# Layer norms of a conv-and-scan kernel's second stage: statistics by broadcast matmuls replaced by transposes and VectorE's batch-norm instructions

## The chip, the cores and the metric

One Trainium2 chip; the kernel runs on one of its cores. The time is device microseconds for one execution of the whole kernel. The engines are TensorE (PE in the profile, its weight loads PEld), VectorE (DVE), ScalarE (ACT), GpSimd (POOL) and SyncE (SP, which issues DMAs).

## The reference

A tensor of 4 images, 192 channels, 64 x 64 positions goes through four layers. Layer 0 is a norm, two Mamba scans and a residual; layer 2 is a dynamic depthwise convolution and layer 3 a windowed sedenion product with an MLP. The change lies in layer 1 alone, cut here to its frame:

```python
t = _ln(transpose(x, (0, 2, 3, 1)), ln1_g, ln1_b)        # norm 1, over the 192 channels
y = _mamba(t.reshape(B, 4096, 192), ...)                 # projections, 3 taps, scan over 4096 positions
x1 = x + back(y)
x2 = x1 + _gelu(batch_norm(depthwise_conv3x3(x1)))
t = _ln(transpose(x2, (0, 2, 3, 1)), ln2_g, ln2_b)       # norm 2, over the 192 channels
out = x2 + back(_gelu(t @ w1 + b1) @ w2 + b2)            # MLP, 192 -> 768 -> 192
# _ln: (x - mean) * rsqrt(var + 1e-5) * g + b, mean and variance over the last axis
```

## The kernel before

`program` runs three stages one after the other. `two_mambas` is layer 0. `mamba_block` is layer 1, called the second stage here. `conv_and_windows` is layers 2 and 3; it is a generator whose first part (batch 0's convolution and norms) is ticked along while the second stage drains.

**Tiles.** The second stage takes 32 tiles, 8 to an image, of 512 positions each. Channels lie on partitions: a tile is [96, 2, 512], two halves of 96 channels. The scan of a tile is 48 steps: 12 groups `k` of four `j`. Each step is one VectorE scan over [128, 512] (L654, `Mamba.step`); ScalarE makes its decay `dA` by an Exp two steps ahead (L648, `decay`, three PSUM buffers); a group begins with a product [128, 2048] (L641), on VectorE, or on GpSimd for groups 3, 7 and 11 ("apart"); it ends with a product by C on GpSimd (L667, `read`), and TensorE gathers the result (L676, `sum`).

**What sets the order.** Each engine works through its own queue in the order of the program, and the program's order is made by the class `Behind`. After each scan step `Behind.tick` issues other work of the stage "behind" the scan. That work is written as generators in five lanes, tried in the order of their numbers: lane 0 the way out of the scan (`back`, with the residual sum into `strip`, L1102) and C's spreading; lane 1 a tile's projections and taps (`front`) and norm 1; lane 2 `tail` (the 3 x 3 convolution as 18 matmul pairs, its gelu, norm 2); lane 3 `end` (the MLP); lane 4 a silu. What a generator yields is a `Piece`: the TensorE time `pe` of the next part, set against a budget of 1.8 a step; the steps to `wait`; flags `after` which it may go; `bank`, since only two PSUM banks are shared by all lanes; `act`, ScalarE's time, set against 1.4 a step; `burst` for long activations (gelu, silu, softplus), which go only two steps before the end of a group that a VectorE product follows; and `lock`, one holder at a time. `Behind.later` puts off the reading of a PSUM bank by one step on ScalarE (`act`) or two on VectorE (`dve`). A deferred reading with an `act` is issued only while the step's ScalarE account is above zero; a Piece that is no burst goes when its `act` is at most 0.84 or the account, whichever is larger, so small pieces go even when the account is negative.

**A norm before** (`NormT.run`, L300 to L356) keeps channels on partitions. TensorE multiplies by a matrix of 1/192 to get the mean on all 96 partitions (`mean`, L307); VectorE subtracts it (L309); ScalarE squares (L316); TensorE sums the squares into [128, 4] (`var`, 8 products with one moving column each, L321); ScalarE adds epsilon (L332) and GpSimd raises to the power -0.5 (L333); TensorE spreads the result back to channels (`rb`, L339); VectorE multiplies (L347); ScalarE applies g and b (L354, twice). On TensorE each f32 product shows as two matmul instructions. The lock is held from after the subtraction to the end of `var`, since `ln_sq` has one buffer.

In each tile there is one norm 1, of the tile two ahead, and one norm 2, at the end of `tail`: 64 norms in all. Norm 2's first product waits for `taken`: `MlpT.run` sets it once the MLP of the tile before has read the one buffer `xn2`. `end` then follows. A `tail` starts when its tile's `back` and the `end` of an older tile are done.

The first stage has a norm of its own (L840 to L890), whose rows are of use below: its input has positions on partitions, ScalarE does its passes (L861) on [128, 192], GpSimd small steps on [128, 4] (L865 to L871), TensorE transposes [128, 96] blocks with one instruction each (L879), and ScalarE reads the result with g and b (L883).

Of the kernel before, what the change touches and what calls it, by code (L numbers as in the profile page):

```python
# [14 lines left out]
F32 = mybir.dt.float32  # L15
AF = mybir.ActivationFunctionType
ALU = mybir.AluOpType
# [5 lines left out]
C = 192  # L23
# [262 lines left out]
class NormT:  # L286


    FIRST = dict(pe=1.7, bank=True)

    def __init__(self, nc, const, work, behind):
        self.nc, self.work, self.behind = nc, work, behind
        self.mean_w = const.tile([CP, CP], F32, name="mean_w")
        nc.vector.memset(self.mean_w, 1.0 / C)
        self.eps = const.tile([128, 1], F32, name="eps")
        nc.vector.memset(self.eps, EPS)
        self.minus_half = const.tile([128, T // 128], F32, name="minus_half")
        nc.vector.memset(self.minus_half, -0.5)
        self.ident = const.tile([128, 128], F32, name="ident")
        make_identity(nc, self.ident)  # L300

    def run(self, x, g, b, d, which):
        nc, behind = self.nc, self.behind
        nq = T // 128
        mean = behind.bank([CP, T], "mean")
        for k in range(2):
            nc.tensor.matmul(mean, self.mean_w, x[:, k, :], start=(k == 0), stop=(k == 1))  # L307
        h = behind.later(
            lambda: nc.vector.tensor_tensor(  # L309
                d, x, mean.unsqueeze(1).broadcast_to([CP, 2, T]), ALU.subtract  # L310
            ),
            dve=True,
        )
        yield Piece(after=[h], wait=3, act=1.05, lock=True)
        sq = self.work.tile([CP, 2, T], F32, name="ln_sq", bufs=1)
        nc.scalar.activation(sq, d, AF.Square)  # L316
        yield Piece(2.5, wait=2, bank=True)
        var = behind.bank([128, nq], "var")
        for q in range(nq):
            for k in range(2):  # L320
                nc.tensor.matmul(  # L321
                    var[:, q : q + 1],
                    sq[:, k, bass.ts(q, 128)],
                    self.mean_w[:, 0:1],
                    start=(k == 0),
                    stop=(k == 1),
                )
        behind.locked = False
        rs = self.work.tile([128, nq], F32, name="ln_rs", tag=f"ln_rs{which}", bufs=1)

        def power():
            nc.scalar.activation(rs, var, AF.Identity, bias=self.eps)  # L332
            nc.gpsimd.tensor_tensor(rs, rs, self.minus_half, ALU.pow)  # L333

        h = behind.later(power, act=0.25)
        yield Piece(1.3, after=[h], wait=4, bank=True)
        rb = behind.bank([CP, T], "rb")
        for q in range(nq):
            nc.tensor.matmul(  # L339
                rb[:, bass.ts(q, 128)],  # L340
                rs[:, q : q + 1].to_broadcast([128, CP]),
                self.ident,
                start=True,
                stop=True,
            )
        h = behind.later(
            lambda: nc.vector.tensor_tensor(  # L347
                d, d, rb.unsqueeze(1).broadcast_to([CP, 2, T]), ALU.mult
            ),
            dve=True,  # L350
        )
        for k in range(2):
            yield Piece(after=[h], wait=0 if k else 3, act=0.8)
            nc.scalar.activation(  # L354
                d[:, k, :], d[:, k, :], AF.Identity, scale=g[:, k : k + 1], bias=b[:, k : k + 1]
            )  # L356
# [655 lines left out]
def mamba_block(tc, x, p96, p96_ap, p128, p128_ap, m_in, ex_aps, out, sums, following):  # L1012
# [4 lines left out]
    with ExitStack() as ctx:  # L1017
# [50 lines left out]
        def norm(u):  # L1068
            xn = u["xn"] = scan.tile([CP, 2, T], F32, name="xn", bufs=1)
            yield from ln.run(u["x"], w["ln1_g"], w["ln1_b"], xn, 1)  # L1070
# [48 lines left out]
        def tail(b, t):  # L1119
# [37 lines left out]
            yield Piece(1.7, bank=True, wait=4, after=[taken[0]])  # L1157
            xn = work.tile([CP, 2, T], F32, name="xn2", tag="xn2", bufs=1)
            yield from ln.run(x2, w["ln2_g"], w["ln2_b"], xn, 2)
            units[b * NT + t]["past"][0] = True  # L1160
            taken[0] = [False]
            behind.add(3, end(b, t, x2, xn, taken[0]), Piece(1.7, bank=True, wait=2))
# [28 lines left out]
        def before(n):  # L1191
            if n + 1 < len(units):
                behind.add(1, front(units[n + 1]), Piece())
            if n + 2 < len(units):
                behind.add(1, norm(units[n + 2]), Piece(1.7, bank=True, after=[units[n + 2]["loaded"]]))
# [15 lines left out]
        behind.add(1, norm(units[0]))  # L1211
        behind.add(1, front(units[0]), Piece())
        behind.add(1, norm(units[1]))
# [633 lines left out]
```

## Time and profile before

| | us |
|---|---|
| median of 3 runs (10560.6 to 10564.75) | 10563.82 |
| span of the profiled execution | 10559.3 |
| second stage, first scan (of 1536) starts | 5324.9 |
| second stage, last scan ends | 8650.5 |
| third stage's first product (L1505) starts | 8899.1 |
| three first tiles of the second stage, together | 292.1 |
| the 28 tiles after them, together | 2944.0 |
| busy in the span: PE / DVE / ACT / POOL | 8657.5 / 8765.6 / 6675.7 / 7932.4 |

The profiled execution's own time is its span and what lies around it; its span is 4.5 us under the median of the runs. A tile's time is from its first scan's start to that of the next tile. In a row of instructions the columns are line, engine, operation, tiles, shape and count, then busy time and mean ns of one, then the engine's idle time before them and what ended it. TensorE's ends are modelled, so that its busy time is not a rate.

### The profile page before, as it was taken

Reading aid. Unit: us, or ns where it says so; the run is one execution under the profiler, and the core shown is the slowest. Engines: PE = TensorE matmul, PEld = TensorE weight load, DVE = VectorE, ACT = ScalarE, POOL = GpSimd, SP = SyncE. Lnnn points to the kernel's source line nnn. Section 1 sums busy time; section 2 is a strip of 40 time slices with the busy share of each in tenths; the row PEclk is TensorE's granted clock in tenths of the full one; section 3 lists DMA queues with packets and bytes.
Section 4 is the critical chain, followed back from the end, with each engine's and each line's share of the span. In section 5 each row is a group of like instructions: output and inputs, shape, how many; then the busy total and the mean of one; then the engine's idle time right before and its main releaser. Section 6 shows DMA issues by size and latency. Waiting matters only on the chain. (4 is left out here: it accounts for less than half of the span.)

```text
span 10559.3 us, 96732 instructions
## 1 busy us (share of the span) xinstructions
PE 8657.5 (82%) x30648; PEld 3478.9 (33%) x30648; DVE 8765.6 (83%) x7569; ACT 6675.7 (63%) x9690; POOL 7932.4 (75%) x3712
## 2 busy tenths in 40 slices
PE   6777777877877777787668888888888996889898
PEld 2222222322322222222223333333333333545555
DVE  7999999999999999999878887887888876555552
ACT  5776777667777667767456676776776653434443
POOL 6999999999999999999778887888888861101100
PEclk7888888888888888888668898998998987999999
DMA  6666666666666666666555554555555543122110
GB/s 163 183 187 180 178 183 186 178 181 188 182 179 183 183 181 180 185 182 179 143 143 148 134 153 131 152 138 143 141 149 135 149 109 74 42 56 59 41 41 19
DMA packets 969559, 1515.09 MB, mean 143 GB/s; under 512 B 244346, under 2 KB 277150, under 8 KB 968534
## 3 DMA queue, kind: packets, MB, share of 16 engines
q1 hardware_dynamic: 968190, 1505.85, 53.5%
q8 instruction: 243, 3.98, 0.2%
q10 hardware_dynamic: 856, 3.05, 0.1%
q14 instruction: 270, 2.21, 0.1%
HBM read 1295.45 MB, written 213.12 MB: 143 GB/s over the span
## 5 line engine op out<-in xcount | busy, mean ns | idle before, releaser
L654 DVE TENSOR_TENSOR_SCAN h<-dA,m_state,h 128x512 f32<-128x512 f32 x3328 | 4041.4, 1266 | 269.8 <-ACT dA L648 207.8
L648 ACT ACTIVATE dA<-dtE,m_A 128x512 f32<-128x512 f32 x4608 | 3101.1, 686 | 1217.6 <-DVE h L654 925.4
L667 POOL TENSOR_TENSOR h<-h,C 128x2048 f32<-128x2048 f32 x832 | 3768.3, 4529 | 71.3 <-ACT C L629 4.0
L641 DVE TENSOR_TENSOR h<-dtxE,B 128x2048 f32<-128x2048 f32 x832 | 1881.7, 2262 | 74.5 <-DMA dtxE<-r_dtx 68.1
L654 DVE TENSOR_TENSOR_SCAN h_apart<-dA,m_state,h_apart 128x512 f32<-128x512 f32 x1280 | 1551.2, 1262 | 199.9 <-ACT dA L648 190.0
L641 POOL TENSOR_TENSOR h_apart<-dtxE,Bs 128x2048 f32<-128x2048 f32 x320 | 1475.5, 4611 | 35.2 <-ACT dA L648 16.2
L667 POOL TENSOR_TENSOR h_apart<-h_apart,C 128x2048 f32<-128x2048 f32 x320 | 1449.7, 4530 | 25.8
L676 PE MATMUL y<-h,gather 128*32 128x512 f32 x6656 | 1040.1, 701 | 486.9 <-POOL h L667 311.5
L1382 POOL TENSOR_TENSOR d<-d,rs 128x512 f32<-128x512 f32 x64 | 86.3, 1348 | 1594.7 <-DVE rs L1381 1573.1
L475 PE MATMUL ps_in<-xT,m_in_w 96*128 96x512 f32 x1536 | 910.1, 742 | 247.9 <-ACT o L918 160.5
L557 PE MATMUL ps_conv<-raw,m_conv 128*128 128x512 f32 x1536 | 732.0, 610 | 8.3 <-ACT raw L482 7.1
L475 PEld LDWEIGHTS ps_in<-xT,m_in_w 96*128 96x128 f32 x1536 | 356.8, 242 | 835.6 <-issue 378.0
L1131 PE MATMUL ps_dw<-strip,dw 96*96 96x512 f32 x1152 | 596.7, 669 | 1.1 <-ACT x L1140 0.9
L504 PE MATMUL ps_dt<-dbl,m_dt_w 12*128 12x512 f32 x576 | 427.7, 847 | 165.9 <-ACT dbl L495 102.5
L676 PE MATMUL y<-h_apart,gather 128*32 128x512 f32 x2560 | 397.8, 698 | 178.7 <-POOL h_apart L667 169.9
L493 PE MATMUL ps_x<-xc,m_pack 128*44 128x512 f32 x576 | 361.8, 779 | 193.1 <-ACT xc L489 178.5
L676 PEld LDWEIGHTS y<-h,gather 128*32 128x32 f32 x6656 | 140.2, 115 | 1122.6 <-issue 574.3
L475 PE MATMUL ps_in<-xn,m_in_w 96*128 96x512 f32 x768 | 403.1, 660 | 114.8 <-ACT z L482 61.7
L1547 PE MATMUL sed_ps<-xn,sed 64*128 64x256 f32 (+3 forms) x2944 | 487.3, 405 | 7.0 <-DVE y L1566 7.0
L514 POOL TENSOR_TENSOR raw<-dt,xc 128x1536 f32<-128x1536 f32 x96 | 325.0, 3386 | 222.9 <-ACT dt L513 180.7
L395 PE MATMUL ps_o<-hid,t 128*96 128x512 f32 x768 | 418.5, 684 | 70.5 <-ACT C L629 63.7
L648 ACT ACT_TABLE_LOAD x345 | 442.6, 1283 | 14.7 <-DMA dtE<-r_dt 8.6
(200 smaller groups left out, 12103.5 us busy)
## 6 DMA issues: line engine op xcount, KB each, us to landing
dtE<-r_dt SPq DMA_DIRECT2D x2304, 256.0 KB, 5.2
dtxE<-r_dtx SPq DMA_DIRECT2D x2304, 256.0 KB, 4.3
r_dt<-dt SPq DMA_DIRECT2D x96, 768.0 KB, 4.0
r_dtx<-raw SPq DMA_DIRECT2D x96, 768.0 KB, 6.5
x<-x SPq DMA_DIRECT2D x64, 384.0 KB, 3.6
img<-x SPq DMA_DIRECT2D x28, 512.0 KB, 8.6
xt<-in_x SPq DMA_DIRECT2D x32, 384.0 KB, 5.4
x<-o SPq DMA_DIRECT2D x32, 384.0 KB, 4.2
```

What stands on the lines that cost most here:

```text
L395: nc.tensor.matmul(ps, self.w2[:, m, bass.ts(k, CP)], h[:, m, :], start=(m == 0), stop=(m == NH - 1),)
L475: nc.tensor.matmul(ps, self.in_w[:, k, bass.ts(e, 128)], xn[:, k, :], start=(k == 0), stop=(k == 1))
L493: nc.tensor.matmul(ps, self.x_w[:, d, :], xc[:, d, :], start=(d == 0), stop=(d == ND - 1))
L504: nc.tensor.matmul(ps, self.dt_w[:, bass.ts(d, 128)], dbl[:RK, :], start=True, stop=True)
L557: nc.tensor.matmul(ps, self.conv[:, d, j, :], raw[:, d, j : j + T], start=(j == 0), stop=(j == K - 1))
L641: engine.tensor_tensor(h, u["rows", k // 2, 1], u[B, k % 2].unsqueeze(1).broadcast_to([128, 4, T]), ALU.mult)
L648: self.nc.scalar.activation(dA, u["rows", k // 2, 0][:, j, :], AF.Exp, scale=self.A[:, k, j : j + 1])
L654: self.nc.vector.tensor_tensor_scan(h[:, j, :], u.pop(("dA", k, j)), h[:, j, :], self.state[:, k, j : j + 1], ALU.mult, ALU.add,)
L667: nc.gpsimd.tensor_tensor(h, h, u["C", k % 2].unsqueeze(1).broadcast_to([128, 4, T]), ALU.mult)
L676: self.nc.tensor.matmul(u["ys"][32 * j : 32 * j + 32, :], self.ex.gather[:, i // 2, :], h[:, j, :], start=(i == 0), stop=(i == 3 and self. ...
L1131: nc.tensor.matmul(ps, dw[:, k, j, :], s[:, k, dy : dy + rows, dx : dx + HW], start=(j == 0), stop=(j == 8),)
L1547: nc.tensor.matmul(out, sed[p, int(h is not None), i ^ position(k, s), cols], xn[b, g][p, c, :], start=group(t) not in begun, stop=left[gr ...
```

## The change

`NormT.run` now turns a tile so that positions are on partitions, takes the statistics there, scales and shifts it there, and turns it back.

- TensorE transposes the eight [96, 128] blocks of the tile into two PSUM banks `ln_t`, and ScalarE copies each ([128, 384]) into `ln_xs` [128, 4, 192].
- VectorE takes the statistics of each 192 channels with four `bn_stats` and four `bn_aggr`, which give mean and variance per position.
- GpSimd makes from them `rs` = (var + eps)^-0.5 and `shift` = -mean * rs, in four operations on [128, 4].
- ScalarE applies them in place in four passes over [128, 192], as its per-partition scale and bias.
- TensorE transposes back into two banks `ln_b`, and ScalarE's reading of them applies g and b (two activations [96, 512]).

The products `mean`, `var` and `rb`, the matrix `mean_w` and VectorE's two passes over the tile are gone. The lock is now held from the first transposes to the second half of the way back. Norm 2's first half may run before `taken`; the way back alone waits for it (`after`), and `xn` and `xn2` are taken when it comes (`to()`). The declared TensorE time of a norm is four pieces of 0.5 where it was 1.7, 2.5 and 1.3. A `tail` that is an image's last now waits for the `end` of the tile two before its own, where it was one older.

```diff
-    FIRST = dict(pe=1.7, bank=True)
+    FIRST = dict(pe=0.5, bank=True, lock=True)
...
-    def run(self, x, g, b, d, which):
-        nc, behind = self.nc, self.behind
+    def run(self, x, g, b, to, which, after=()):
+
+        nc, behind, ident = self.nc, self.behind, self.ident
         nq = T // 128
-        mean = behind.bank([CP, T], "mean")
+        xs = self.work.tile([128, nq, C], F32, name="ln_xs", bufs=1)
+        made = []
+        for part in range(0, nq, 2):
+            if part:
+                yield Piece(0.5, bank=True)
+            ps = behind.bank([128, 2, C], "ln_t")
+            for q in range(2):
+                for k in range(2):
+                    nc.tensor.transpose(
+                        ps[:, q, bass.ts(k, CP)], x[:, k, bass.ts(part + q, 128)], ident[:CP, :CP]
+                    )
+            made.append(
+                behind.later(lambda part=part, ps=ps: nc.scalar.copy(xs[:, part : part + 2, :], ps), act=0.5)
+            )
+        yield Piece(after=made, wait=2)
...
+        for q in range(nq):
+            nc.vector.bn_stats(sums[:, q].rearrange("p a b -> p (a b)"), xs[:, q, :])
+        for q in range(nq):
+            nc.vector.bn_aggr(mv[:, q, :], sums[:, q].rearrange("p a b -> p (a b)"))
+        yield Piece(wait=1)
+        nc.gpsimd.tensor_scalar(rs, mv[:, :, 1], EPS, None, ALU.add)
+        nc.gpsimd.tensor_tensor(rs, rs, self.minus_half, ALU.pow)
+        nc.gpsimd.tensor_tensor(shift, mv[:, :, 0], rs, ALU.mult)
+        nc.gpsimd.tensor_scalar(shift, shift, -1.0, None, ALU.mult)
+        yield Piece(wait=3)
+        for q in range(nq):
+            yield Piece(act=0.55)
+            nc.scalar.activation(
+                xs[:, q, :], xs[:, q, :], AF.Identity, scale=rs[:, q : q + 1], bias=shift[:, q : q + 1]
+            )
         for k in range(2):
-            nc.tensor.matmul(mean, self.mean_w, x[:, k, :], start=(k == 0), stop=(k == 1))
...
+            yield Piece(0.5, bank=True, wait=0 if k else 2, after=after)
+            out = out if k else to()
+            ps = behind.bank([CP, T], "ln_b")
+            for q in range(nq):
+                nc.tensor.transpose(ps[:, bass.ts(q, 128)], xs[:, q, bass.ts(k, CP)], ident)
+            h = behind.later(
+                lambda k=k, ps=ps, out=out: nc.scalar.activation(
+                    out[:, k, :], ps, AF.Identity, scale=g[:, k : k + 1], bias=b[:, k : k + 1]
+                ),
+                act=0.75,
+            )
         behind.locked = False
...
-            yield Piece(1.7, bank=True, wait=4, after=[taken[0]])
-            xn = work.tile([CP, 2, T], F32, name="xn2", tag="xn2", bufs=1)
-            yield from ln.run(x2, w["ln2_g"], w["ln2_b"], xn, 2)
+            yield Piece(wait=4, **ln.FIRST)
...
+            yield from ln.run(x2, w["ln2_g"], w["ln2_b"], to, 2, [taken[0]])
...
-            first = [u["done"]] + ([units[n - 3]["ended"]] if n > 2 else [])
             for t2 in ([t - 1] if t else []) + ([t] if t == NT - 1 else []):
+                old = b * NT + t2 - 2
+                first = [u["done"]] + ([units[old]["ended"]] if old >= 0 else [])
                 behind.add(2, tail(b, t2), Piece(2.6, bank=True, after=first, wait=2))
```

More of the change, by code (lines that the diff above doesn't have):

```diff
@@ L286 @@
 class NormT:
-    FIRST = dict(pe=1.7, bank=True)
+    FIRST = dict(pe=0.5, bank=True, lock=True)
     def __init__(self, nc, const, work, behind):
         self.nc, self.work, self.behind = nc, work, behind
-        self.mean_w = const.tile([CP, CP], F32, name="mean_w")
-        nc.vector.memset(self.mean_w, 1.0 / C)
         self.eps = const.tile([128, 1], F32, name="eps")
@@ L300, in __init__ @@
         make_identity(nc, self.ident)
-    def run(self, x, g, b, d, which):
-        nc, behind = self.nc, self.behind
+    def run(self, x, g, b, to, which, after=()):
+        nc, behind, ident = self.nc, self.behind, self.ident
         nq = T // 128
-        mean = behind.bank([CP, T], "mean")
-        for k in range(2):
[L307 to L327, printed above, removed]
-        behind.locked = False
[L329 to L356, printed above, removed]
@@ new lines, in run @@
+        yield Piece(after=made, wait=2)
+        sums = self.work.tile([128, nq, 2, 3], F32, name="ln_sums", tag=f"ln_sums{which}", bufs=1)
+        mv = self.work.tile([128, nq, 2], F32, name="ln_mv", tag=f"ln_mv{which}", bufs=1)
+        rs = self.work.tile([128, nq], F32, name="ln_rs", tag=f"ln_rs{which}", bufs=1)
+        shift = self.work.tile([128, nq], F32, name="ln_shift", tag=f"ln_shift{which}", bufs=1)
+        for q in range(nq):
+            nc.vector.bn_stats(sums[:, q].rearrange("p a b -> p (a b)"), xs[:, q, :])
@@ L359 @@
+        behind.locked = False
+        yield Piece(after=[h])
 class MlpT:
@@ L1068, in norm, with to @@
         def norm(u):
-            xn = u["xn"] = scan.tile([CP, 2, T], F32, name="xn", bufs=1)
-            yield from ln.run(u["x"], w["ln1_g"], w["ln1_b"], xn, 1)
+            def to():
+                u["xn"] = scan.tile([CP, 2, T], F32, name="xn", bufs=1)
+                return u["xn"]
+            yield from ln.run(u["x"], w["ln1_g"], w["ln1_b"], to, 1)
         def front(u):
@@ L1156, in tail, with to @@
                 )
-            yield Piece(1.7, bank=True, wait=4, after=[taken[0]])
-            xn = work.tile([CP, 2, T], F32, name="xn2", tag="xn2", bufs=1)
-            yield from ln.run(x2, w["ln2_g"], w["ln2_b"], xn, 2)
+            yield Piece(wait=4, **ln.FIRST)
+            xn = []
+            def to():
+                xn.append(work.tile([CP, 2, T], F32, name="xn2", tag="xn2", bufs=1))
+                return xn[0]
+            yield from ln.run(x2, w["ln2_g"], w["ln2_b"], to, 2, [taken[0]])
             units[b * NT + t]["past"][0] = True
             taken[0] = [False]
-            behind.add(3, end(b, t, x2, xn, taken[0]), Piece(1.7, bank=True, wait=2))
+            behind.add(3, end(b, t, x2, xn[0], taken[0]), Piece(1.7, bank=True, wait=2))
         def end(b, t, x2, xn, taken):
@@ L1194, in before @@
             if n + 2 < len(units):
-                behind.add(1, norm(units[n + 2]), Piece(1.7, bank=True, after=[units[n + 2]["loaded"]]))
+                behind.add(1, norm(units[n + 2]), Piece(after=[units[n + 2]["loaded"]], **ln.FIRST))
         def after(n):
@@ L1210, in mamba_block @@
             load(u)
-        behind.add(1, norm(units[0]))
+        behind.add(1, norm(units[0]), Piece(**ln.FIRST))
         behind.add(1, front(units[0]), Piece())
-        behind.add(1, norm(units[1]))
+        behind.add(1, norm(units[1]), Piece(**ln.FIRST))
         Scans(nc, stream, behind).run()
```

## The prediction

> **What bounds the kernel now.** I read the page's slices first, then engine busy time tile by tile in the second stage, then the waits there, then the rows of the norms. The second stage is slices 21 to 33 of 40:
>
> ```profile
> PE   6777777877877777787668888888888996889898
> DVE  7999999999999999999878887887888876555552
> POOL 6999999999999999999778887888888861101100
> PEclk7888888888888888888668898998998987999999
> ```
>
> VectorE and GpSimd fill the first stage; in the second they drop to eight tenths while TensorE rises. Two plain tiles, and the two at an image's border:
>
> ```profile
> core 0: us, PE busy (x) PEld busy (x) DVE busy (x) ACT busy (x) POOL busy (x), PEclk, DMA share, GB/s
> 7411.80:7514.20 102.40, 91.50 (x292) 32.64 (x292) 86.90 (x70) 73.32 (x99) 88.18 (x45) 0.93 0.56 147
> ...
> 7616.70:7719.10 102.40, 91.47 (x292) 32.63 (x292) 86.91 (x71) 73.34 (x99) 88.22 (x45) 0.93 0.53 146
> ...
> 8026.60:8138.00 111.40, 97.81 (x292) 35.73 (x292) 87.31 (x70) 72.59 (x98) 89.61 (x45) 0.88 0.50 134
> 8138.00:8251.50 113.50, 101.01 (x292) 34.58 (x292) 87.14 (x71) 73.24 (x100) 88.30 (x45) 0.85 0.49 132
> ```
>
> No engine is full, but TensorE is nearest to it, and where two tails meet only its time grows. VectorE is idle 15.5 us of 102.4. Its waits over five tiles (engine and line, what ended the wait, us, times, longest):
>
> ```profile
> DVE h_apart L654 <- ACT dA L648: 25.6, 15, 3.3
> DVE strip L1102 <- PE ps_out L1093: 21.6, 10, 3.6
> DVE h L654 <- ACT dA L648: 15.5, 24, 1.5
> DVE xn L309 <- PE mean L307: 7.2, 10, 0.8
> DVE xn L347 <- PE rb L339: 6.8, 5, 1.4
> ```
>
> Per tile: 2.8 at the norms, 4.3 at `strip`, 8.2 for a late `dA`. ScalarE is late mostly behind TensorE: over the same tiles it waits 22.9 for `ps_dw`, 17.4 for `ps_h`, 17.2 for `ps_C`. I put 6.2 of the 8.2 down to that, and 2.0 to long activations, above all the MLP's gelu near a tile's end. So TensorE's lateness costs about 10.5 us a tile (4.3 + 6.2), the norms' own waits 2.8.
>
> The plain tile repeats to 0.03 us. [...] 102.40 is 30.0 windows, an image of eight tiles (839.67 us) 246.0, and the clock of 0.93 is 28 of 30. The tile is locked to that window.
>
> **The change part by part.** Rows of the norms, and of the first stage's norm, which has the operations that come in:
>
> ```profile
> L307 PE MATMUL mean<-x,mean_w 96*96 96x512 f32 x256 | 136.0, 658 | 19.3 <-DMA x<-x 13.7 <-ACT z L482 5.3 <-ACT hid L381 0.2
> L321 PE MATMUL var<-mean_w,ln_sq 96*128 96x1 f32 x1024 | 143.9, 270 | 32.6 <-ACT xc L585 14.6 <-ACT ln_sq L316 10.0 <-DVE x L1166 7.9
> L339 PE MATMUL rb<-ident,ln_rs 128*96 128x128 f32 x512 | 83.5, 315 | 37.3 <-POOL ln_rs L333 29.4 <-ACT xc L585 5.6 <-POOL m_halo L469 1.5
> L879 PE MATMUL ps_t<-ident,xs 128*96 128x128 f32 x256 | 41.2, 282 | 21.6 <-ACT xs L861 21.6
> ```
>
> ```profile
> L861 ACT ACTIVATE xs<-xt,shift,rs 128x192 f32<-128x192 f32 x128 | 67.8, 532 | 4.6 <-POOL m_halo L469 4.6
> ```
>
> *TensorE.* Out: (136.0 + 143.9 + 83.5) / 64 = 5.7 us busy per norm. In: 16 transposes at 41.2 / 256 = 0.16, 2.6. The eight forward ones have another shape ([96, 128] in); by start-to-start times (0.11 for L879, 0.09 to 0.11 for the 96-column L910) all 16 cost 1.5 to 2.6. Saved: 3.1 to 4.2 per norm, 6.2 to 8.4 a tile; I take 6.6. TensorE then has 85 us of work in a tile.
>
> *VectorE.* Out: 1.216 + 1.212 = 2.43. In: four `bn_stats` and four `bn_aggr`, which no run here shows. [...] Low end: 249 ns for each statistics instruction and 62 (a [128, 4] memset, L832) for each aggregate, 1.2. High end: 553 (two passes, the [128, 384] row of L995) and 186 (L447), 3.0. I take 2.1: -0.7 a tile, between -2.5 and +1.1.
>
> *VectorE's waits.* 2.8 a tile go with L309 and L347. The statistics wait for ScalarE's copies, issued a step or more before them: nothing taken, up to 2 if TensorE is late.
>
> *ScalarE.* Out: 1.045 + 0.255 + 2 x 0.807 = 2.91. In: two copies of 384 columns, between 0.315 (192, L918) and 0.581 (512, L482), 0.475 each; four passes at 0.532; two readings at 0.762 (L883): 4.6. So +3.4 a tile, to 76.7. As a sum it is covered by ScalarE's 29 idle us; where it lands is another matter. In the built program's order, once settled, norm 2's four passes come at step 33 directly behind the MLP's gelu, since small pieces go on a negative account; norm 1's come at step 46, a step behind a silu. After a `dA`, step 33's queue is table load 1.28, gelu 2.77, passes 2.13, table load 1.28, next `dA` 0.69: 8.15. VectorE has for it about half a scan, two scans at 1.18 and a product 2.26, so 5.1: a stall of 3.0. At step 46 it is table 1.28, silu 1.49, table 1.28, `dA`, passes 2.13, `dA` = 7.6 against 6.3: 1.3. The gelu's own 1.45 and some 0.5 at the end of a tile (timeline) go. Net +2.4. [...]
>
> *GpSimd.* Out 1.013; in 0.192 + 1.103 + 0.225 + 0.234 = 1.75 (L869, L870, L871, L865). +1.5 a tile, to 89.7. Behind them in the queue stands the next product by C; it bounds nothing while tiles are above 95. At step 43 they stand behind a 4.5 us product, and the passes at step 46 may wait 0 to 1.4 for them.
>
> *No DMA* is added, and none moves out of its order behind `strip` and the store.
>
> *TensorE's relief.* Of 10.5 us caused by its lateness I take half, 5.2: its work falls by 6.6, but after step 33 the account is so negative (-6.5) that the reading of `z` is put off five steps with both banks held, so it idles there and starts again at a low clock. Ends: nothing to all of 10.5.
>
> A plain tile: 102.4 - 0.7 - 2.8 + 2.4 - 5.2 = 96.1. With the ends of the relief it is 101.3 to 90.8. If the lock stays, the next window multiple upward is 29, 99.0 us; I forecast that.
>
> *Border tiles.* The settled order in the built program is the same for all tiles, borders too: 28 tiles at 99.0 = 2772 against 2944.0, **-172**. The first three, with little TensorE work (292.1): -3.
>
> *Hand-over.* Last scan to the third stage's first product is 248.6 now. In the new order a tile more is open at the last scan: an MLP (24 products of 0.86, 20.6 on TensorE, with gelu and readings some 35) and a norm. TensorE is busy 178 of 249 there and batch 0's preparation runs beside it. +15, between -10 and +60.
>
> Sum: 10559.3 - 172 - 3 + 15 = 10,399 as a span; the median of the runs lay 4.5 above it: **10,404**.
>
> **Rivals.**
> - *28 windows, or no lock.* For it: 96.1 is my own sum before rounding, and a tile with only a norm and a front took 93.5. 28 x 95.6 = 2676, -268: 10,308.
> - *30 windows hold.* VectorE's relief is eaten by stalls at steps 33 and 46 until 102.4 catches it again; only the border tiles gain. For it: the tile ahead of a border, whose work stands in another order, took 102.7, nearly the same. 28 x 102.4 = 2867, -77: 10,499.
> - *No measurable change.* 30 windows and the hand-over's upper end, +60 for +15: 10,544; within 10,543 to 10,585.
> - *Slower: ScalarE's passes become the bound.* At steps 33 and 46 they hold the next `dA` back, longer if GpSimd's small steps come late. It decides once a tile passes 104.7 (2944 less the other terms' 12, over 28), that is with 8.6 us more of stalls than my 96.1. At 31 windows, 105.8: +19 - 3 + 15, 10,595. Against it: ScalarE is idle 29 us, and its waits for L347 (16.5 over five tiles) go as well.
>
> **How the numbers follow.** Chances: 97 to 101 a tile 0.46; at or under 97 0.22; 102.4 0.17; no change 0.05; slower 0.10. About 0.2% (21 us) is what a measurement of this kernel can tell from no change. Faster 0.85, same 0.05, slower 0.10. The likeliest case's own range is 10,365 to 10,435. For 8 in 10 I take it with most of the two neighbours: 10,295 to 10,515.
>
> **What would show it.** Right: plain and border tiles alike near 99; TensorE near 85 a tile; VectorE without waits at its norm work; a wait of about 3 us of the scan at step 36 for `dA` behind L648's table load. Wrong: a tile still 102.4 (relief worth nothing); VectorE busy above 88 (`bn_stats` slow); ScalarE idle before the four passes until GpSimd (late `rs`); a hand-over over 300.

## The result and the profile after

The changed kernel takes as long as the one before: 10560.22 us median (10550.46 to 10564.19), ratio 0.9998 with a 95% interval of 0.999 to 1.0006. The forecast was 10404, with 10295 as the low end and 10515 as the high one. The profiled execution is the fastest of twelve (span 10548.6, time 10550.46); its stages add up like this:

| us | before | after | forecast |
|---|---|---|---|
| first scan of the second stage starts | 5324.9 | 5318.2 | same |
| first three tiles | 292.1 | 284.2 | -3 |
| 28 tiles after them | 2944.0 | 2917.6 | -172 |
| last tile | 89.5 | 93.5 | in the hand-over |
| last scan's end to the third stage's first product | 248.6 | 264.6 | +15 |
| that product to the end | 1660.2 | 1670.6 | same |

So 26 of the expected 172 us came, and they went again at the last tile, the hand-over and in batch 0's part of the third stage. The first row is unchanged code: over the profiles of all the kernels below it lies between 5313.8 and 5325.1, so that a difference of this size needn't be the change's. The page's slices show TensorE's busy tenths and its clock in 40 equal parts of the span:

```profile
PE   7777777877877777777668888888888886889898
PEclk7888888888888888888668888898898887999999
```

In slices 21 to 33 TensorE's two nines of before are gone, and of its clock's six nines two are left. In the profile of the changed kernel the granted clock is whole (1.00) and half (0.50) by turns, in 798 stretches, and in that of the kernel before in 778. In both, any two changes lie a whole multiple of 3.413 us apart, and the shortest stretch is 3.413 us (as 48.24 to 51.65 of the changed kernel, 0.50 between 1.00 and 1.00). A "window", here as in the prediction and the expectations, is this measured step; "half clock", "low-clock" and "cold" mean a window at half. Tile by tile, two plain tiles and then the two at a border (span, busy us of each engine with instructions, granted clock, DMA):

```profile
core 0: us, PE busy (x) PEld busy (x) DVE busy (x) ACT busy (x) POOL busy (x), PEclk, DMA share, GB/s
6862.70:6966.70 104.00, 88.78 (x269) 30.18 (x268) 84.95 (x84) 76.50 (x107) 89.69 (x52) 0.89 0.55 144
6966.70:7070.90 104.20, 89.00 (x269) 30.16 (x268) 84.85 (x83) 75.96 (x107) 89.63 (x52) 0.89 0.54 144
...
7173.40:7277.40 104.00, 90.38 (x269) 30.80 (x268) 84.85 (x83) 76.42 (x107) 89.48 (x51) 0.89 0.54 144
7277.40:7381.60 104.20, 88.90 (x269) 30.17 (x268) 84.87 (x83) 76.02 (x107) 89.53 (x51) 0.89 0.56 144
```

The border is gone: 104.0 and 104.2 where it was 111.4 and 113.5. The plain tile got longer, 102.4 to 104.1, although VectorE has 2.0 us less to do and TensorE issues less. TensorE's busy time fell by 2.2 only, over these four tiles, while its clock fell from 0.93 to 0.89. Two such tiles together (208.2) take 61.0 windows, where each took 30.0 (102.40); a shorter tile of 101.8 to 102.9 comes in between now and then.

VectorE's waits over five tiles (what waited, what ended it, us, times, longest):

```profile
DVE h L649 <- ACT dA L643: 32.3, 12, 4.4
DVE strip L1100 <- PE ps_out L1091: 16.2, 5, 5.0
DVE x L1169 <- PE ps_o L390: 13.9, 10, 1.7
DVE h_apart L649 <- ACT dA L643: 13.2, 10, 2.4
DVE ln_sums L324 <- ACT ln_xs L316: 11.3, 10, 1.7
```

The scan's waits for `dA` are 45.5 for 41.1, fewer and longer. `strip` fell from 21.6 to 16.2. The norms' waits of before (14.0) are replaced by those for ScalarE's copies (11.3). New is a wait for the products of the MLP's second layer (`ps_o`), 13.9. The statistics themselves cost what the forecast said, 2.0 us a norm (4 x 0.347 + 4 x 0.154) for 2.1. From the groups of the second stage (busy, mean ns; idle before and its releaser):

```profile
L324 DVE BATCH_NORM_STATS2 ln_sums<-ln_xs 128x6 f32<-128x192 f32 x236 | 67.9, 347 | 59.8 <-ACT ln_xs L316 59.8
L326 DVE BATCH_NORM_AGGREGATE ln_mv<-ln_sums 128x2 f32<-128x6 f32 x236 | 21.4, 154 | 0.0
```

The longest waits lie around steps 31 to 38. One tile's timeline there, TensorE first, then ScalarE (start, us, operation, count, idle before it):

```profile
7339.10 3.70 PE L371 MATMUL ps_h<-xn,t 96*128 96x512 f32 x8
...
7345.59 3.48 PE L371 MATMUL ps_h<-xn,t 96*128 96x512 f32 x4 [1.80 <-ACT hid L376]
...
7362.00 3.78 PE L470 MATMUL ps_in<-xn,m_in_w 96*128 96x512 f32 x4 [8.29 <-ACT z L477]
```

```profile
7349.11 0.69 ACT L376 ACTIVATE hid<-ps_h,t 128x512 f32<-128x512 f32 x1 [2.39 <-PE ps_h L371]
...
7351.69 2.77 ACT L383 ACTIVATE hid<-hid 128x3072 f32<-128x3072 f32 x1
7354.37 1.84 ACT L335 ACTIVATE ln_xs<-ln_xs,ln_shift,ln_rs 128x192 f32<-128x192 f32 x4
```

Eight instructions of the MLP's first layer take 3.70; the next four, after a gap of 1.80, take 3.48, at half clock (0.50 from 7345.94 to 7349.35). ScalarE waits 2.39 for them. Behind that wait and one `dA` stand the gelu (L383), the four passes (L335) and two table loads of 1.28, and only then comes the `dA` after it. TensorE meanwhile idles 8.29 and starts cold again (0.50 from 7356.18 to 7366.42).

### The profile page after: what moved, and what is told of

Its sections match the earlier page's. It is cut to its first block, busy times and chain, and to the rows that moved or that the text cites. A ratio compares the mean times of both kernels' runs of the same rounds, so it can differ in the third digit from the quotient of the medians.

```text
span 10548.6 us, 96012 instructions
## 1 busy us (share of the span) xinstructions
PE 8493.3 (81%) x29880; PEld 3358.6 (32%) x29880; DVE 8701.6 (82%) x7952; ACT 6760.0 (64%) x9942; POOL 7974.7 (76%) x3904
## 5 line engine op out<-in xcount | busy, mean ns | idle before, releaser
L671 PE MATMUL y<-h,gather 128*32 128x512 f32 x6656 | 1069.8, 720 | 519.9 <-POOL h L662 347.1
L470 PE MATMUL ps_in<-xn,m_in_w 96*128 96x512 f32 x768 | 468.9, 757 | 260.6 <-ACT z L477 176.8
L1129 PE MATMUL ps_dw<-strip,dw 96*96 96x512 f32 x1152 | 541.7, 620 | 0.3 <-ACT ln_xs L316 0.2
L371 PE MATMUL ps_h<-xn,t 96*128 96x512 f32 x768 | 443.4, 725 | 58.2 <-ACT hid L376 44.6
L661 POOL COPY m_state<-h 128x4 f32<-128x4 f32 x832 | 158.5, 190 | 405.4 <-DVE h L649 395.3
```

The source lines that it names most:

```text
L371: nc.tensor.matmul(ps, self.w1[:, k, bass.ts(m, 128)], x[:, k, :], start=(k == 0), stop=(k == 1))
L470: nc.tensor.matmul(ps, self.in_w[:, k, bass.ts(e, 128)], xn[:, k, :], start=(k == 0), stop=(k == 1))
L671: self.nc.tensor.matmul(u["ys"][32 * j : 32 * j + 32, :], self.ex.gather[:, i // 2, :], h[:, j, :], start=(i == 0), stop=(i == 3 and self. ...
L1129: nc.tensor.matmul(ps, dw[:, k, j, :], s[:, k, dy : dy + rows, dx : dx + HW], start=(j == 0), stop=(j == 8),)
```

## The experiments

"Settled tile" is the mean time of tiles 12 to 29 (counted from 0) of the profiled execution: 104.68 before (102.40 without the borders), 103.64 after. "Clock" is TensorE's mean granted clock over the same tiles. All ratios are to runs of the kernel before that were taken beside that experiment, with a 95% interval.

**1. The tail's rule alone**, in the kernel before:

```diff
-            first = [u["done"]] + ([units[n - 3]["ended"]] if n > 2 else [])
             for t2 in ([t - 1] if t else []) + ([t] if t == NT - 1 else []):
+                old = b * NT + t2 - 2
+                first = [u["done"]] + ([units[old]["ended"]] if old >= 0 else [])
```

> The kernel before with one line of the change alone: the tail waits for the end of the tile before it by its own number (b*NT+t2-2) instead of n-3. In the built program every tile then has the order of a plain tile, at the images' borders too. If the border tiles' 111.4 and 113.4 us are a matter of order, they become 102.4 each: three borders, 3 x 20.0 = 60 less, 10,500, with the hand-over unchanged at about 249. If they come from two tails' work falling into one tile, the time stays at 10,560. And if the order is what gave the change its -26 in 28 tiles, the norm by transposes itself is a loss of about 35 us there.

10497.34 us, 0.9942 (0.9928 to 0.9955). Every settled tile is a plain one, at a border too:

```profile
8082.10:8184.50 102.40, 91.47 (x292) 32.62 (x292) 86.90 (x70) 73.35 (x99) 88.24 (x45) 0.93 0.56 147
```

The 28 tiles take 2882.6, 61 less, and the hand-over and what follows don't move (248.6 and 1660.2). The border's extra time was a matter of order alone, and this one line takes it away, a gain of 63 without the new norm. Against that kernel the changed one, which has the line too, loses 63: 35 in the 28 tiles, the rest mostly behind them.

**2. Less TensorE work, order unchanged.** The kernel before with `mean` and `var` made of one half of the channels; it leaves the other half out of both statistics:

```diff
-        for k in range(2):
-            nc.tensor.matmul(mean, self.mean_w, x[:, k, :], start=(k == 0), stop=(k == 1))
+        nc.tensor.matmul(mean, self.mean_w, x[:, 0, :], start=True, stop=True)
...
-            for k in range(2):
-                nc.tensor.matmul(
...
+            nc.tensor.matmul(
+                var[:, q : q + 1],
+                sq[:, 0, bass.ts(q, 128)],
+                self.mean_w[:, 0:1],
+                start=True,
+                stop=True,
+            )
```

> The kernel before with the products for mean and variance made of one half of the channels only, which leaves the other half out of both statistics; the order of all instructions stays. TensorE loses about (136.0 + 143.9) / 128 = 2.2 us per norm, 4.4 a tile, and nothing else changes. If TensorE's amount of work sets the tile at the order before (my forecast's step: half of the lateness goes with 6.6 us), the tile falls by 3 to 4 us, to 99.0: 28 x -3.4 = -95, 10,465. If its order and the locked clock set it, the tile stays at 102.4 and the time within 20 of 10,560.

10556.72, 0.9997 (0.9988 to 1.0005): no gain. Two plain tiles:

```profile
7402.70:7508.20 105.50, 91.73 (x272) 31.06 (x272) 86.82 (x71) 73.29 (x99) 88.32 (x45) 0.89 0.54 142
7508.20:7614.60 106.40, 93.29 (x272) 31.07 (x272) 87.07 (x71) 72.99 (x99) 88.14 (x45) 0.87 0.52 141
```

There are twenty matmul records fewer, in the same order, and TensorE is *longer* busy (92.5 for 91.5) at a clock of 0.88 for 0.93. The plain tile went from 102.4 to about 106. The two at a border, 111.6 and 101.7 for 111.4 and 113.5, give most of that back: the settled tile is 105.83 for 104.68. So the forecast's relief, a fall of the plain tile, has the wrong sign here, and in the kernel's time less work brings nothing. Over five plain tiles VectorE's waits for `dA` are 66.1 for 41.1.

**3. Without the second norm's passes** (its output is then neither centred nor scaled to unit variance), and **4. with every transpose twice**, both in the changed kernel and in its order:

```diff
             yield Piece(act=0.55)
+            if which == 2:
+                continue
```

```diff
-                for k in range(2):
+                for k in (0, 0, 1, 1):
...
-            for q in range(nq):
+            for q in [q for q in range(nq) for _ in range(2)]:
```

> The changed kernel without ScalarE's four scale-and-shift passes of the second norm, so that this norm's division by the deviation and the subtraction of the mean are left out; the order stays. These passes stand behind the MLP's gelu at step 33. If they are what eats the gain, the stall of scan 36 (4.4 us, with 2.1 at scan 35) falls by about 2.1 and the restart of TensorE comes 2 us earlier: the tile falls by 2 to 3 us, 28 x -2.5 = -70, 10,490. If TensorE's idle stretch and its low clock there set the tile, under 1 us a tile: 10,535 to 10,560.

> The changed kernel with every transpose of the norms issued twice; nothing else changes, nor the order. That is about 32 x 0.11 = 3.5 us more TensorE work a tile. If TensorE's amount of work still sets the tile, the tile grows by 2 to 3.5 us: +60 to +100, 10,620 to 10,660. If its order and cold clock set it, the time stays within 20 of 10,560, or falls where the added work keeps the clock up.

Without the passes: 10510.88, 0.9954 (0.9941 to 0.9968); settled tile 102.35, 1.3 less, 60.0 windows for two. The five tiles' longest wait for `dA` falls from 4.4 to 2.6:

```profile
DVE h L651 <- ACT dA L645: 21.5, 11, 2.6
```

The time is 49 us under the changed kernel's. That lies between the two cases that were written down, under 1 us a tile and 2 to 3. The wait at scan 36 falls as it was expected to, but `strip` takes part of it back (23.2 for 16.2). Transposes twice: 10553.19, 0.9994 (0.9985 to 1.0002); the clock rises to 0.91 and the settled tile is 103.34. Three and a half us of added work cost nothing.

**5. The new form for the first norm only.** The second has its old code back; the two forms share a scratch buffer. The tail's rule is the new one:

```diff
-            yield Piece(wait=4, **ln.FIRST)
...
-            yield from ln.run(x2, w["ln2_g"], w["ln2_b"], to, 2, [taken[0]])
+            yield Piece(1.7, bank=True, wait=4, after=[taken[0]])
+            xn = [work.tile([CP, 2, T], F32, name="xn2", tag="xn2", bufs=1)]
+            yield from lo.run(x2, w["ln2_g"], w["ln2_b"], xn[0], 2)    # lo: the norm of before
```

> The changed kernel with transposes for the first norm only; the second has its products, subtractions and multiplications of before back. The first norm's scratch and the second's share one buffer. The order of the rest changes with it: the gelu comes at step 13 and no passes stand behind it. Beside the kernel with the tail's rule alone (10,497) it has 1.2 us less VectorE work, 3.3 less TensorE work, 1.7 more ScalarE work a tile. If the second norm's passes behind the gelu eat the gain, the first norm's form costs nothing or brings some: tile 100 to 102.4, 10,430 to 10,500. If the form itself costs, by its copies, its wait and a lower clock, half of the loss of 63 shows: tile near 103.5, about 10,530.

10568.44, 1.0011 (1.0004 to 1.0018); settled tile 105.81, three tiles 93.0 windows, clock 0.87. The loss against experiment 1 is 71, all of it and more with half the change. In this kernel the gelu comes at step 13, with no passes behind it. So that clump isn't the only thing that costs, and the parts don't add. The order is another one too, so this doesn't price the first norm's form by itself.

**6. VectorE's statistics twice** (each `bn_stats` issued again):

```diff
-        for q in range(nq):
+        for q in [q for q in range(nq) for _ in range(2)]:
             nc.vector.bn_stats(sums[:, q].rearrange("p a b -> p (a b)"), xs[:, q, :])
```

> The changed kernel with each statistics instruction of VectorE issued twice; nothing else changes, nor the order. That is 8 x 0.26 to 0.36 = 2.1 to 2.9 us more VectorE work a tile, at two places. If VectorE's sequence and the releases it gives set the tile, the tile grows by 1.5 to 2.5: +40 to +70, 10,600 to 10,630. If the 19 us in which VectorE is idle take it up (the chain through TensorE's and ScalarE's queues sets the tile), the time stays within 20 of 10,560.

10565.44, 1.0009 (1.0001 to 1.0018): 5 us over the changed kernel by the medians, some 12 by the ratios, whose intervals overlap. Added in full it would be 2.8 x 28 = 79. A tile:

```profile
7385.30:7489.50 104.20, 88.82 (x269) 30.02 (x269) 87.72 (x90) 75.92 (x107) 89.50 (x51) 0.89 0.55 144
```

VectorE has 87.7 for 84.9 to do and the tile is the same 104.2; the settled tile is 104.04 for 103.64. VectorE's time isn't what sets it, in this order.

**7, 8 and 12. The same instructions in other orders**: the passes planned at no ScalarE time; two steps for three ahead of them; the reading of `z` planned at no ScalarE time:

```diff
-            yield Piece(act=0.55)
+            yield Piece(act=0.0)
```

```diff
         nc.gpsimd.tensor_scalar(shift, shift, -1.0, None, ALU.mult)
-        yield Piece(wait=3)
+        yield Piece(wait=2)
```

```diff
-            return behind.later(lambda: nc.scalar.copy(to, ps))
+            return behind.later(lambda: nc.scalar.copy(to, ps), act=0.65 * (not self.summed))
```

> The changed kernel with the four passes planned at no ScalarE time (0.0 for 0.55 each); the same instructions in another order. The passes then stand at steps 11 or 12 and 43 or 44, ahead of the gelu or some steps from it, the account doesn't fall to -6.5, and z's reading is not put off for five steps. If that place in the order is what ate the gain, the tile falls to 99 to 101 and the time to 10,400 to 10,480, the hand-over being shorter too. If the form of the norm costs in any order, the tile is 102 to 104 and the time over 10,500.

> The changed kernel with two steps in place of three between GpSimd's small instructions and the passes; the same instructions, in another order again: the first norm's passes at step 43, the second's some steps from the gelu, tails later in the tile. It is a second sample of another order: if the place of the passes counts it lies with the kernel that plans the passes at no time, within 30 of it and under 10,500; if it is over 10,540, what decides is some other part of the order.

> The changed kernel with the reading of z planned at no ScalarE time, so that it isn't put off when the account is negative; the same instructions in another order, settled from the first tile on. z is read a step after its products (33 and 34 in place of 38 and 39), and the passes stand at steps 27 and 44, away from the gelu at 33. If the reading of z put off behind gelu and passes, with TensorE idle and cold after it, is what ate the gain, the tile is 99 to 101: 10,400 to 10,480. If any order of this form costs (as in the two other orders run), the tile is 104 to 110: 10,550 to 10,720.

10702.36 (1.0137, 1.0122 to 1.0152), 10739.17 (1.0171, 1.0156 to 1.0186) and 10564.48 (1.0004, 0.9996 to 1.0013). My theory at that point was that the gain is lost where `z` is read late behind gelu and passes. It fell with these three: in 7 and 8 gelu and passes stand at steps 12 to 19 and `z` at 34 to 36; in 12 `z` still follows the gelu, but without the passes between. None is faster. Their settled tiles are 110.1, 113.0 and 104.7, at clocks of 0.85, 0.83 and 0.90. Their orders repeat after 129.0 windows for four tiles, 66 or 67 for two, and 92.0 for three.

**9, 10 and 11. More TensorE work where it idles.** At each step in which the planner gives TensorE nothing, the products of a bank that still waits for its reading (`z`'s, or the MLP's first layer) are issued again into that bank:

```diff
+    def warm(self):
+        self.again = [a for a in self.again if not a[0][0]]
+        if self.quiet and self.again:
+            self.again[0][1]()
+        elif self.quiet and self.dummy and not self.held:
+            self.dummy(self.psum.tile([128, T], F32, name="ps_warm", tag="mm"))
...
+            behind.again.append((made[-1], products))
...
+            done = behind.later(lambda: nc.scalar.copy(to, ps))
+            behind.again.append((done, lambda: projected(e, ps)))
...
             self.behind.tick(self.edge(i + self.AHEAD, n))
+            if m.summed and i < n:
+                self.behind.warm()
```

Experiment 9 has no `dummy`, an unused product that nothing reads; 10 has it; 11 is experiment 1 with both.

> The changed kernel, in the same order, with the products of z and of the MLP's first layer issued again into their own held bank at each step in which TensorE is given nothing while such a bank waits for its reading: steps 30 and 33 to 37 of a tile, about 1.7 us each. It adds some 10 us of TensorE work a tile, just where TensorE idles 8.3 us and its clock falls to half for three windows (steps 35 to 38). If low-clock windows set the tile (about 1.5 us each, over all orders run so far), three fewer of seven take 3 to 4.5 us off: tile near 100, 10,440 to 10,480. If the late reading itself (ScalarE's queue) sets it, the tile stays at 104 or gets longer by what a repeat holds the reading back: 10,560 to 10,620.

> As the kernel with the repeats, and besides two unused products (weights by weights, into a bank that nothing reads) at steps 12 and 19, where no bank is held and TensorE is given nothing. TensorE's low-clock windows at steps 6 to 10 and 26 aren't touched. By the clock: the same as the kernel with the repeats alone, within 25. If unused products hold up what is behind them: 20 to 60 above it.

> The kernel before with the tail's rule alone and TensorE filled in the same way: unused products at steps 25, 31 and 45 of a tile, repeats at 34 and 37. Its plain tile of 102.4 has four low-clock windows of 30, at steps 46 to 1 (two), 11 and 25. If low-clock windows set the tile, two fewer give 99.0 (29 windows): 28 x -3.4 = -95 against 10,497, so 10,400. If the order of the work sets it, 10,490 to 10,530.

The repeats: 10490.09, 0.9935 (0.992 to 0.9949). Some 10 us of work added to each tile make the kernel 70 us faster. With unused products as well 10588.51 (1.0028, 1.0017 to 1.0039), and experiment 1 with them 10623.67 (1.0061, 1.0046 to 1.0076). In experiment 10 the clock rises to 0.97, and still the settled tile is 102.61 for 101.26, and the first three tiles take 305.8 for 287.4. In experiment 11 four windows of a tile are at half clock as in experiment 1, and the tile is 105.81, one window longer. So a high clock isn't enough, and added work doesn't always raise it. By the code an unused product takes a bank in its turn and a place in TensorE's queue; that this is its cost wasn't tested.

Windows of 3.41 us from steps 32 to 38 of one tile, the changed kernel:

```profile
7345.23:7348.65 3.42, 3.06 (x4) 1.31 (x5) 3.04 (x3) 1.50 (x3) 3.00 (x7) 0.60 0.97 249
...
7355.47:7358.89 3.42, 0.00 (x0) 0.00 (x0) 0.64 (x1) 3.39 (x6) 3.42 (x2) 0.60 1.02 262
...
7362.30:7365.71 3.41, 3.41 (x4) 0.88 (x4) 3.41 (x3) 1.21 (x2) 1.85 (x2) 0.50 0.99 251
```

and the same place with the repeats:

```profile
7304.03:7307.45 3.42, 3.42 (x8) 1.56 (x9) 2.75 (x4) 2.52 (x5) 3.00 (x6) 1.00 0.99 251
...
7310.86:7314.27 3.41, 3.41 (x14) 1.02 (x13) 0.00 (x0) 3.39 (x6) 3.33 (x2) 1.00 0.52 135
```

With the repeats the clock (third number from the end) is whole throughout. Two places differ: the first line, in which the last four instructions of the MLP's first layer run, and the stretch after the gelu. (The stretches of the first fence start a little beside the clock's own windows, so a line can mix whole and half.)

**13 and 17. Which place?** `z`'s repeats alone (the line for the MLP's bank left out), and the MLP's alone (the line for `z` left out):

```diff
-            behind.again.append((made[-1], products))
```

```diff
-            behind.again.append((done, lambda: projected(e, ps)))
```

> The changed kernel with the repeats of z's products alone (steps 33 to 37), without the one of the MLP's first layer at step 30. If the clock after the idle stretch behind the gelu is the place, it keeps at least 55 of the 70 us that the repeats at all six steps brought: 10,490 to 10,505. If the gain came from step 30, where the MLP's products hold the bank, it falls back to 10,540 or more.

> The changed kernel with only the repeat of the MLP's first layer at step 30 (none of z's). Both kinds of repeat gave 10,490, z's alone 10,549, none 10,560. If the chain that sets the tile is the MLP's first layer in a low-clock window at step 32, hid, gelu and dA behind it, this one repeat, 1.7 us of added TensorE work a tile, wins most of the 59 between them, even with TensorE idle and cold at steps 35 to 38: 10,495 to 10,515. If both stretches are needed together, 10,535 to 10,560.

| repeats | us | ratio (interval) | settled tile | clock |
|---|---|---|---|---|
| none | 10560.22 | 0.9998 (0.999 to 1.0006) | 103.64 | 0.890 |
| `z`'s, steps 33 to 37 | 10548.72 | 0.9991 (0.9984 to 0.9998) | 103.27 | 0.932 |
| MLP's, step 30 | 10523.29 | 0.9964 (0.9952 to 0.9977) | 102.40 | 0.909 |
| both | 10490.09 | 0.9935 (0.992 to 0.9949) | 101.26 | 0.953 |

I had the place wrong, and then half right. Filling the long idle stretch, which catches the eye, brings 11 us, and its interval overlaps that of no repeats: TensorE is cold there, but little waits for it (in the changed kernel ScalarE's reading of `z`, 10.2 us over five tiles, where its reading of the MLP's first layer waits 25.4). One product pair repeated at step 30 wins 37, though it leaves that stretch idle and cold:

```profile
7321.04 5.42 PE L384 MATMUL ps_h<-xn,t 96*128 96x512 f32 x12
...
7327.54 1.99 PE L384 MATMUL ps_h<-xn,t 96*128 96x512 f32 x4
...
7342.45 2.93 PE L486 MATMUL ps_in<-xn,m_in_w 96*128 96x512 f32 x3 [6.93 <-ACT z L493]
```

The last four instructions of the MLP's first layer now run at a clock of 1.00 and take 1.99 for 3.48, and ScalarE waits 0.89 for them where it waited 2.39. That is 1.5 us earlier for gelu, passes and the next `dA`; VectorE's wait at scan 35, of 2.1 to 2.4 us, falls to 0.7, and the settled tile is 1.24 shorter. Both together win more than their sum, 70 for 48 us and 2.4 for 1.6 in the settled tile, so neither accounts for it alone; the intervals of the times by themselves leave the sum open.

**14. Repeats and transposes twice** (experiments 4 and 9 in one):

> The changed kernel with the repeats (10,490) and with every transpose twice, 3.5 us more TensorE work a tile, now with the clock held up through the idle stretch. If TensorE's amount of work counts once its clock is up, the tile grows by 1 to 3.5 us: 10,520 to 10,590. If it doesn't count in either state, within 20 of 10,490.

10521.86, 0.9962 (0.9947 to 0.9977), 32 over experiment 9; settled tile 102.41 for 101.26. It is the same addition that cost nothing in experiment 4; here it costs 1.15 us a tile for 3.5 us of work, at the same clock (0.95). Either the amount of work counts once the clock is held up, or the tile has fallen onto 30.0 windows, as it does here and not in experiment 9; no run tells the two apart.

**15 and 16. Repeats in the other order, and one more repeat.** Experiment 1 with the repeats (no unused products), and experiment 9 with `ps_x`'s products again at step 21:

```diff
         h = behind.later(lambda ps=ps: nc.scalar.copy(dbl, ps))
+        behind.again.append((h, products))
```

> The kernel before with the tail's rule and the repeats alone, no unused products: in its order they fall on steps 34 and 37, where its clock is already full. If the clock is what the repeats act by, nothing is gained here: 10,490 to 10,530, and the new norm with the repeats isn't slower than the old one with them. If the repeats help in some other way (readings later, banks turned in another order), it gains as much as the changed kernel did: about 10,430.

> The changed kernel with the repeats and, besides, the products of the projection by x_w again at step 21, just ahead of the low-clock windows that are left at steps 25 to 28. If they are warm then, the tile loses another 1 to 2 us: 10,430 to 10,470. If the repeat (2.6 us) only delays the reading behind it, as the unused products did, 10,500 to 10,560.

The first: 10484.99, 0.9932 (0.9916 to 0.9949), the fastest median of all, but its interval overlaps those of experiments 1 and 9. Its settled tile is 102.40 as in experiment 1, where the clock is already whole at steps 34 and 37; the 12 us lie in tiles 2 to 6 and at the stage's end. In these five tiles 34 windows are at half clock where experiment 1 has 48. So the repeats act where they lift the clock, and the new norm with them is about level with the old one with them. The second: 10512.27, 0.9955 (0.994 to 0.9969). The clock rises to 0.96 and the settled tile to 101.99. That fits a repeat (2.6 us) that gets in the way of what is behind it, as was written, but that this is the cause isn't shown.

**18. The passes spread**, one to a step, with the repeats:

```diff
-            yield Piece(act=0.55)
+            yield Piece(act=0.55, wait=(1 if q else 2) if which == 2 else 0)
```

> The changed kernel with the repeats (10,490) and the second norm's four passes one to a step (35 to 38) in place of all behind the gelu at step 33; up to there one of its two settled tile orders is the same, later pieces move a little and the hand-over may be longer. If the clump of four behind the gelu costs (scan 36 waits 4.4 us in all runs of this order, 2.6 without the four passes), that wait falls to about 2.5 and the tile by 1 to 2: 10,440 to 10,480. If the wait is made up by other lateness, 10,490 to 10,560.

10650.81, 1.0086 (1.0071 to 1.0101). In the tile whose order is the old one up to step 34 the wait at scan 36 is 2.6 for 4.4, as expected; in the next, whose order is another, one wait for `dA` is 9.1. The settled tiles are 105 and 110. In this planner the shorter wait came only with an order that costs more.

## Why the prediction was wrong

The step that failed is **TensorE's relief**: "of 10.5 us caused by its lateness I take half, 5.2", with "nothing to all of 10.5" as its ends. It took lateness to shrink with the work. The runs show that it doesn't. With the relief and ScalarE's stalls (+2.4) it made VectorE's waits for `strip` and `dA` 9.7 us a tile where they were 12.5. They are 12.3, and 2.8 of waiting for the MLP's products came on top. At an unchanged order, 4.4 us less work made the plain tile some 3.5 us *longer* and brought the kernel nothing (experiment 2); 3.5 us more left the tile alone (experiment 4); and 10 us more, in the right places, made it 2.4 shorter (experiment 9).

What TensorE saved here was given back through its clock. The number of windows at half clock in a tile, worked out from tile time and clock, is 4.0 in the plain tile of before, 7.3 in the settled tile of experiment 2 and 6.7 in that of the changed kernel; four instructions of the MLP's first layer took nearly twice as long in such a window (3.48 us for 1.99). At one place, the MLP's first layer at step 30, experiment 17 shows the whole chain from the clock to the tile; at the others it is inferred from the clock alone. The forecast knew that TensorE "idles there and starts again at a low clock" and used it only to shrink the gain. The low end had to go below nothing.

Of the forecast's 172 us, 77 were the borders' extra time and 95 the plain tile's way from 102.4 to 99.0. The first part came, 61, by the line for the tail alone (experiment 1). In place of the second, the 28 tiles are 35 longer than with that line and the old norm.

Point by point:

- *VectorE, -0.7.* Busy time fell by 2.0. The 347 and 154 ns of an instruction lie between the forecast's ends (249 to 553, rows of L995 in the kernel before, and 62 to 186), and 2.0 a norm near the 2.1 taken between them, but those of a row overlap: `bn_stats` start 0.26 apart and `bn_aggr` 0.07. The saving was counted in full, and experiment 6 shows that 2.8 us of VectorE work is worth 0.4 us of a tile. VectorE's idle time rose from 15.5 to 19.3 instead.
- *The norms' waits, -2.8.* They went, and 2.3 came back as waits for the copies. "nothing taken" was the wrong choice, and "up to 2 if TensorE is late" nearly the size but not the reason: before its copies ScalarE waits only 4.2 us for the transposes over some 30 tiles, so they stand behind other work in its own queue.
- *ScalarE, +3.4 of work, a stall of 3.0 at step 36 and 1.3 at step 46.* Work +2.9. The stall at scans 35 and 36 is 6.5 (2.1 and 4.4): the late MLP products stand ahead of the gelu that I counted from. None over 0.4 shows at step 46.
- *GpSimd, +1.5, no bound.* Right: +1.4, and the four passes' wait for it over five tiles is 1.1.
- *A whole number of windows per tile.* The "lock" is shown as a period alone (102.40 us is 30.0 windows before), and as one of a single tile it was wrong in form: the whole number is that of several tiles. The changed kernel settles to 61.0 windows for two (208.2 us), not 29 each.
- *Border tiles alike.* Right, but it is the tail's rule that does it (experiment 1), not the norm.
- *Hand-over +15.* 16, and for the reason given: behind the last scan the trace has 96 matmul records of each MLP layer, where it had 71 and 72, which is one tile's MLP more. In the changed norm's orders 7 and 8, with 69 to 72, the hand-over is 245.7 and 242.7. Not foreseen: batch 0's part of the third stage is 10.4 longer, and the last tile 4. Experiments 5, 7, 8 and 12, in other orders, have 1656 to 1662 there for 1670.6, but 18, in another order too, has 1675. Why isn't known.
- *The rivals.* "No measurable change" was given 0.05 for a hand-over of +60; the time fell there for another reason. The mechanism nearest to what happened is that of "30 windows hold", stalls at step 33 that eat the relief; it missed that they could eat more than all of it.

In its own order the changed kernel's settled tile is 1.24 us longer than that of experiment 1. One chain ahead of scans 35 and 36 accounts for that much: shorten it at either end, by the four passes (3) or by the late products (17), and the tile is 102.35 or 102.40. Both kernels then repeat after 60.0 windows for two tiles; whether that set how far they fell isn't shown.

What stays open: which pieces of the new form make its orders slow. Half the change (5) costs as much as the whole, three other orders cost as much or more, and each has its cold windows in other places. What transposes do to the clock wasn't tested by itself; it rose with transposes added (experiment 4, 0.89 to 0.91). The changed norm with the old rule for the tail wasn't run.

## What to carry over

Where a planner's order and a clock that moves with it (0.83 to 0.97 over the orders and fillings run here) stand between an engine's work and the time, price a change by the gaps that it leaves, not by the work that it saves, and let the range go below nothing. Test the amount of work directly, by halving or doubling it at an unchanged order, before a forecast rests on it; and when a change has several edits, price the one-line edit to the order by itself, since here that line alone won 63 us and the whole change nothing. A long idle stretch isn't the place to mend unless something waits for its end: here one repeated product pair, ahead of a gelu that `dA` stood behind, won over three times what filling the longest gap did (1.24 for 0.37 us a tile).

## What the runs showed of the hardware

- With less work TensorE's clock fell so far that it was busy for longer: with 20 fewer matmul records a tile the clock went from 0.93 to 0.88 and busy time from 91.5 to 92.5 (experiment 2). With a product pair issued again in an idle step the products behind it ran at a clock of 1.00 (experiment 17). Four f32 instructions of 512 columns took 1.99 us at the whole clock there and 3.48 at half clock in the changed kernel.
- In most of these orders the settled period was a whole number of the clock's windows (3.413 us, measured in the profiles of both kernels), over one tile or several: 30.0 for one tile (102.40 us; before's plain tiles, and experiments 1, 14, 15), 31.0 (105.81 us; 11), 60.0 for two (3, 17), 61.0 for two (208.2 us; 6, and the changed kernel but for its shorter tiles), 90.0, 92.0 and 93.0 for three (16 in most places, 12, 5), 121.0 and 129.0 for four (4, 7). In experiments 9 and 13 it is no whole number (about 59.1 for two, 120.8 for four), though the clock is as high in 14 and 16, where it is. What decides isn't shown.
- The number of half-clock windows in a tile didn't by itself give its time. Experiment 13 has a clock of 0.932 and a tile of 103.27, experiment 17 has 0.909 and 102.40: it counted which work lay in them.
- In the changed kernel `bn_stats` on [128, 192] f32 took 347 ns and `bn_aggr` from [128, 6] 154 ns; in a row of four they started 260 and 66 ns apart.
